# Squares, sums, taps and next norms placed elsewhere in the attention pair loop

## The chip, the cores and the metric

The kernel runs on one core of a Trainium2 chip. A core has five engines that each work through a queue of their own in order: TensorE (PE in the profile, its weight loads PEld), VectorE (DVE), ScalarE (ACT), GpSimd (POOL) and SyncE (SP), which issues the transfers. An engine stands still while the instruction at the head of its queue waits for another engine. The metric is the device time of one run in microseconds (us); the median of three runs is given.

## What is computed

The input is a batch of four images with 256 channels and 64 x 64 pixels. Four layers follow one another, each as `x = x + layer(group_norm(x))`. Layers 0 and 1 are attention layers, 2 and 3 Mamba layers. Cut to what matters here:

```python
def _gn(v, G=32, eps=1e-5):          # v's last axis is an image axis: 32 groups of 2 of its lines
    ...
    return ((g - m) / jnp.sqrt(s + eps)).reshape(v.shape)

# an attention layer
y = mhsa(x, ...)                     # a gated scan along the image
# ssa: 64 windows of 8 x 8 pixels; each window attends to its 4 most similar windows
attn = softmax(qh * SCALE @ kh)      # 8 heads, 64 queries x 256 keys per window
out = attn @ vh
lepe = depthwise_conv3x3(v_img) + lepe_b
out = (out + lepe) @ wo_w.T + wo_b
```

So a group of the norm is two neighbouring lines of the image (along its last axis) with all channels, and a strip of eight lines holds four groups and needs four means and four variances. The kernel keeps the image with these lines as its rows, and they are called rows below.

## The kernel before, in words

The partitions hold channels (2 x 128). The image is worked on in eight strips of eight rows. For each image the function `attention_layers` runs layer 0 and then layer 1, each as a scan phase (`scan_phase`) and a window phase (`window_phase`); the two Mamba layers follow. The order on every engine is the order in which the Python code emits instructions; nothing reorders them.

The window phase is a loop over 32 pairs of windows, `i = 4*sj + a`, with `sj` the strip and `a` from 0 to 3 the pair in it. A pair is handled in two halves h = 0 and 1 (its parity steps). Per half TensorE computes scores (L538), VectorE takes their minimum (L550), ScalarE the exponentials (L561, four per half, each with a sum), VectorE the reciprocal (L573), GpSimd four normalising multiplications (L576), TensorE transposes (L589), VectorE and ScalarE copy the transposes out (L600, L602), and TensorE forms the values (L615), a pair later. `own_rows` adds them into the image `vimg` on VectorE (L626). The halves of consecutive pairs are interleaved.

Around these, further work is hung into the loop:

- `project(s, m)`: the output projection of the finished strip `sj - 1`, at a = 1 and a = 2: four matmuls (L232) and, at the pair's end, an add into x on VectorE (L636). At pairs 19, 20, 23 and 24 a query projection of the same size stands there, which ScalarE copies out (L298).
- `taps`: the depthwise convolution of strips 6 and 7 on GpSimd, one step in each half of pairs 0 to 25: mostly a multiplication (`weigh`, L253) and then an addition (`add`, L256). The product lies in a buffer with the tag "sq", of which there is one.
- `dve_taps`: nine taps of strip 6 (channels 0 to 127) on VectorE (L268 the first, L270 the others), one at the end of each pair from 2 to 10.
- In layer 0 (`nxt` is set): the steps of the next layer's norm for strips 0 and 1 (`gn`): sums on VectorE (L143), their columns on TensorE (L134), the centring on GpSimd (L151), the square on ScalarE (L156, into the "sq" buffer), its reduction on VectorE (L160), the columns again, and the scaling (L167 on VectorE; L168, a power, and L172 on GpSimd).
- In layer 1: the variances of all eight strips (`stats`), which the Mamba layer needs: sums on VectorE (L200), columns on TensorE (L195), the mean on VectorE (L206), four squares on ScalarE (L215, one per group, each with a sum), columns, and a copy (L221). Strips 0 to 6 are hung into the loop, strip 7 follows it.

The dictionaries `mids` and `ends` hold what runs in the middle of a pair (after the first half's exponentials and the second half's minimum, before the second half's exponentials) and at its very end (before the next pair's first exponentials). `plan` fills them from a list of places; what falls past the last pair is returned in `left` and run after the loop, in an order written out by hand. In this phase all projections and all columns share the one PSUM buffer with the tag "mm".

Of the kernel before, what the change touches and what calls it, by code (L numbers as in the profile page):

```python
# [8 lines left out]
F32 = mybir.dt.float32  # L9
BF16 = mybir.dt.bfloat16  # L10
U32 = mybir.dt.uint32
AF = mybir.ActivationFunctionType
# [6 lines left out]
P = 128  # L19
NB = 4  # L20
C = 256
S = 64
# [22 lines left out]
class Net:  # L45
# [33 lines left out]
    def attention_layers(self, x, w_drams, v_drams):  # L79
        tc, nc = self.tc, self.nc  # L80
        with ExitStack() as ctx:
# [3 lines left out]
            norm = ctx.enter_context(tc.tile_pool(name="at_n", bufs=2, reuse_waits="tile"))  # L85
# [27 lines left out]
            def load_scan_weights(lay):  # L113
                lay["wa"] = wp.tile([P, 2, 4 * C], F32, tag="wa", name="att_wa")
                nc.sync.dma_start(lay["wa"], lay["w"][:, :, 0 : 4 * C])
# [73 lines left out]
            def stats(s, psum):  # L189
                xs = x.rearrange("p (c h w) -> p c w h", c=2, w=S)[:, :, strip[s], :]  # L190
                box = {}

                def columns(tag, part):
                    box[tag] = psum().tile([P, NT], F32, tag="mm", name=f"gn_{tag}")
                    nc.tensor.matmul(box[tag][:, 0:4], self.one_gn, part, start=True, stop=True)  # L195

                def sums():
                    box["s1"] = self.small.tile([P, 4], F32, tag="gn_s1", name="gn_s1")
                    xr = x.rearrange("p (n w) -> p n w", w=S)[:, :, strip[s]]
                    nc.vector.tensor_reduce(  # L200
                        box["s1"], xr.rearrange("p n (g t) -> p g n t", t=2), AX.XY, ALU.add
                    )

                def mean():
                    box["mean"] = self.small.tile([P, 4], F32, tag="gn_mean", name="gn_mean")
                    nc.vector.tensor_scalar(  # L206
                        box["mean"], box["pm"][:, 0:4], -1.0, None, ALU.mult
                    )

                def squares():  # L210
                    box["s2"] = self.small.tile([P, 4], F32, tag="gn_s2", name="gn_s2")
                    sq = norm.tile([P, 2, 8, S], F32, tag="xn", name="gn_sq")
                    for g in range(4):
                        two = slice(2 * g, 2 * g + 2)
                        nc.scalar.activation(  # L215
                            sq[:, :, two], xs[:, :, two], AF.Square,
                            bias=box["mean"][:, g : g + 1], accum_out=box["s2"][:, g : g + 1],
                        )

                def variance():  # L220
                    nc.vector.tensor_copy(self.gvar[:, 4 * s : 4 * s + 4], box["pv"][:, 0:4])  # L221

                return (
                    sums, lambda: columns("pm", box["s1"]), mean, squares,
                    lambda: columns("pv", box["s2"]), variance,
                )

# [241 lines left out]
            def window_phase(lay, work, psum, idx, nxt):  # L469
# [128 lines left out]
                def turned(h, j):  # L598
                    if j == 0:
                        nc.vector.tensor_copy(pts[h][0], pt[h][0])  # L600
                    else:
                        nc.scalar.activation(pts[h][1], pt[h][1], AF.Copy)  # L602
# [52 lines left out]
                dve_taps = lepe(lay, NW - 2)[:9]  # L655

                mids, ends, left = {}, {}, []
# [8 lines left out]
                if nxt:  # L666
                    load_scan_weights(nxt)
                    for s in range(2):
                        i = 10 + s
                        plan(gn(nxt, s, lambda: psum), (ends, i), (ends, i + 1), (mids, i + 2),  # L670
                             (ends, i + 2), (mids, i + 3), (ends, i + 5), (mids, i + 6))
                else:

                    for s in range(NW - 1):
                        i = 4 * s + 6
                        last = i + 6 if s < 5 else i + 3
                        plan(stats(s, lambda: psum), (ends, i), (ends, i + 1), (mids, i + 2),
                             (ends, i + 2), (ends, last), (mids, last + 1))
                for i in range(n_pair):
                    sj, a = divmod(i, 4)  # L680
                    add = evict = None
                    exps(i, 0, (0, 1))
                    if i:
                        scores(i, 1)
                        turned(0, 0)
                        turned(0, 1)
                        turn(i - 1, 1)
                        smallest(i, 1)
                    exps(i, 0, (2, 3))
                    for t in mids.get(i, ()):  # L690
                        t()
                    if i == 0:
                        for f in early:
                            f()
                    normalise(i, 0)
                    for t in taps[2 * i : 2 * i + 1]:
                        t()
                    if a == 3 and sj + 2 in (NW - 2, NW - 1):
                        evict = query(lay, sj + 2, 0, psum)
                    elif a == 0 and sj + 1 in (NW - 2, NW - 1):  # L700
                        evict = query(lay, sj + 1, 1, psum)
                    elif a in (1, 2) and sj:
                        add = project(sj - 1, a - 1, psum)
                    exps(i, 1, (0, 1))
                    scores(i + 1, 0)
                    if i:
                        turned(1, 0)
                        turned(1, 1)
                        values(i - 1)
                    turn(i, 0)  # L710
                    smallest(i + 1, 0)
                    exps(i, 1, (2, 3))
                    normalise(i, 1)
                    if i:
                        own_rows(i - 1)
                    for t in taps[2 * i + 1 : 2 * i + 2]:
                        t()
                    for t in dve_taps[i - 2 : i - 1] if i > 1 else ():
                        t()
                    if add:  # L720
                        add()
                    if evict:
                        evict()
                    gather(i + 3)
                    if a == 0 and 1 < sj + 1 < NW - 2:
                        double(sj + 1)
                    elif a == 1 and sj + 1 in (NW - 2, NW - 1):
                        double(sj + 1)
                    indices(i + 4)
                    for t in ends.get(i, ()):  # L730
                        t()
# [15 lines left out]
                box = {}  # L747
# [3 lines left out]
            with tc.tile_pool(name="at_p0", bufs=2, space=PSUM, reuse_waits="tile") as psum:  # L751
                box = {"psum": psum}
                g = [gn_four(layers[0], s, lambda: box["psum"]) for s in range(2)]
                for step in (g[0][0], g[1][0], g[0][1], g[0][2], g[0][3], g[1][1], g[1][2]):
                    step()
            tail = g[1][3:]
            for i, lay in enumerate(layers):
                with tc.tile_pool(name=f"at_a{i}", bufs=1, reuse_waits="tile") as work, tc.tile_pool(
                    name=f"at_p{i}", bufs=5, space=PSUM, reuse_waits="tile"
                ) as psum:  # L760
                    box["psum"] = psum
                    scan_phase(lay, work, psum, tail)
                    idx = routing(lay, work, psum)
                    taps = lepe(lay, NW - 3, psum)[:9]
                    for s in range(2, 5):
                        evicts = [query(lay, s, m, psum, nc.vector) for m in range(2)]
                        for t in taps[3 * s - 6 : 3 * s - 3]:
                            t()
                        for evict in evicts:
                            evict()  # L770
                    for t in lepe(lay, NW - 3, pool=True)[17:]:
                        t()
                with tc.tile_pool(name=f"at_c{i}", bufs=1, reuse_waits="tile") as work, tc.tile_pool(
                    name=f"at_q{i}", bufs=1, space=PSUM, reuse_waits="tile"
                ) as psum:
                    nxt = layers[i + 1] if i + 1 < len(layers) else None
                    box, tail, left = window_phase(lay, work, psum, idx, nxt)
                    if nxt is None:
                        box["psum"] = psum
                        g = stats(NW - 1, lambda: psum)  # L780
                        for t in (left[0], tail[0], left[1], tail[1], g[0], left[2], left[3], *g[1:]):
                            t()


# [1379 lines left out]
```

## Time and profile before

| what | value |
|---|---|
| median of three runs | 12,002.51 us (11,993.68 to 12,006.19) |
| the profiled execution, its own time | 11,985.03 us |
| its span | 11,983.3 us |
| busy: TensorE, VectorE, ScalarE, GpSimd | 84%, 82%, 58%, 74% of the span |
| granted TensorE clock, mean | 0.932 |
| squares of the variances (L215) | 128 x 0.766 us |
| GpSimd tap additions (L256) | 256 x 1.184 us |
| VectorE taps in the pair loop (L270) | 64 x 0.969 us |

A row of the costliest groups reads: line, engine, operation, tiles written and read, shapes, count; then busy time in us and mean ns of one; then how long the engine stood idle just before these instructions and what ended most of it. A row of a view of stretches reads: the stretch in us from the span's start, its length, busy time of each engine with its number of instructions, the granted TensorE clock (1.00 is full speed), and the transfers' share. A row of the timeline reads: start, duration, engine, line, operation, and in brackets the idle time before it with its releaser. A row of the waits reads: who waited for whom, total us, times, longest.

### The profile page before, as it was taken

The page shows a single profiled execution, that of the slowest core. Times are in us where ns is not written, and L with a number is a line of the kernel's source. Part 1 is how long each engine was busy: PE and PEld are TensorE (multiplying, and loading weights), DVE is VectorE, ACT ScalarE, POOL GpSimd, SP SyncE. Part 2 cuts the span into 40 slices and gives each one's busy share as a digit, 9 for nine tenths or more (in the row PEclk, how much of TensorE's full clock was granted, in tenths as well). Part 3 has the DMA queues.
Part 4 walks back from the last instruction along what each step waited for, and adds up shares of the span by engine and source line. Part 5 has one row for each costly group of instructions (what it writes and reads, how often), then busy time and mean ns, then how long its engine had stood idle before and what let it go on. Part 6 is the DMA issues. An engine that isn't in the chain of part 4 may idle for free.

```text
span 11983.3 us, 192241 instructions
## 1 busy us (share of the span) xinstructions
PE 10083.2 (84%) x71104; PEld 5778.2 (48%) x71104; DVE 9833.8 (82%) x8350; ACT 7002.3 (58%) x13096; POOL 8811.5 (74%) x6054
## 2 busy tenths in 40 slices
PE   8998887777899888777799988877778998887777
PEld 4564554444455455444445645544444554554444
DVE  6677998998666799899866779989986667998998
ACT  4555555776455555477645555547764555554776
POOL 4666886898456688689745668868984666887897
PEclk9999998999999899899999989989999999998999
DMA  3343454454334355445433434444543343454454
GB/s 96 100 126 134 174 175 149 169 180 160 92 98 127 134 173 177 145 169 182 159 90 99 128 132 173 174 148 167 180 160 91 100 127 135 173 176 146 169 176 154
DMA packets 682506, 1742.10 MB, mean 145 GB/s; under 512 B 88896, under 2 KB 194896, under 8 KB 681312
## 3 DMA queue, kind: packets, MB, share of 16 engines
q1 hardware_dynamic: 676448, 1721.41, 43.1%
q10 hardware_dynamic: 5120, 8.39, 0.3%
q8 instruction: 563, 9.22, 0.3%
q14 instruction: 375, 3.07, 0.1%
HBM read 1601.52 MB, written 94.39 MB: 142 GB/s over the span
## 4 chain that ended last, share of the span: by engine, by line
DVE 23%; PE 23%; ACT 8%; issue 5%; POOL 4%; DMA 1%; SPq 0%; DVEq 0%; POOLq 0%; ACTq 0%
DVE h L1002 13%; DVE pb L996 5%; PE conv_ps L232 4%; PE y L954 4%; PE u_ps L1291 3%; ACT da L938 2%; PE pb L926 1%; PE u_ps L1664 1%; POOL pr L576 1%; PE sc L538 1%; DVE lp L270 1%; PE pt_ps L589 1%; ACT dap L938 1%; PE z_ps L1316 1%; POOL hc L1008 1%
## 5 line engine op out<-in xcount | busy, mean ns | idle before, releaser
L1008 POOL TENSOR_TENSOR hc<-h,cb 128x1024 f32<-128x1024 f32 x2056 | 4809.6, 2350 | 806.4 <-DVE h L1002 350.9
L1002 DVE TENSOR_TENSOR_SCAN h<-da,m_state,pb 128x1024 f32<-128x1024 f32 x1248 | 2920.6, 2340 | 161.4 <-DVE pb L996 2.4
L954 PE MATMUL y<-ident,hc 128*128 128x128 f32 x16384 | 2333.6, 290 | 408.0 <-POOL hc L1008 340.9
L954 PEld LDWEIGHTS y<-ident,hc 128*128 128x128 f32 x16384 | 2034.5, 150 | 1124.9 <-POOL hc L1008 577.0
L996 DVE TENSOR_TENSOR pb<-du,pb 128x1024 f32<-128x1024 f32 x1672 | 2025.4, 1211 | 113.4 <-PE pb L926 110.9
L938 ACT ACTIVATE da<-delta,m_v 128x1024 f32<-128x1024 f32 x1672 | 1899.5, 1141 | 135.5 <-DVE h L1002 118.3
L926 PE MATMUL pb<-m_parts,pick 128*128 128x512 bf16 x3312 | 1078.2, 410 | 846.1 <-DVE h L1002 777.6
L576 POOL TENSOR_SCALAR pr<-pr,sm,zero 128x256 f32<-128x256 f32 x2048 | 1136.5, 569 | 476.8 <-DVE sm L573 475.8
L561 ACT ACTIVATE pr<-sc,mn 128x256 f32<-128x256 f32 x2048 | 955.9, 482 | 647.5 <-DVE sm L573 480.9
L926 PEld LDWEIGHTS <-pick 128*128 128x128 bf16 x3312 | 263.1, 101 | 1787.4 <-DVE h L1002 981.2
L550 DVE TENSOR_REDUCE mn<-sc 128x4 f32<-128x1024 f32 x512 | 627.9, 1228 | 550.0 <-PE sc L538 547.2
L1002 DVE TENSOR_TENSOR_SCAN h<-da,pb 128x1024 f32<-128x1024 f32 x424 | 969.5, 2287 | 55.1 <-DVE pb L996 0.9
L912 POOL TENSOR_TENSOR bb<-du,bb 128x1024 f32<-128x1024 f32 x376 | 888.6, 2363 | 88.8 <-DMA bb<-m_cd 84.0
L589 PE MATMUL pt_ps<-ident,pr 128*128 128x128 f32 x4096 | 705.4, 304 | 144.3 <-POOL pr L576 51.1
L1002 DVE TENSOR_TENSOR_SCAN h<-dap,m_state,bb 128x1024 f32<-128x1024 f32 x288 | 672.4, 2335 | 65.1 <-ACT dap L938 45.9
L232 PE MATMUL conv_ps<-att_y,att_wb 128*128 128x512 f32 x1536 | 683.3, 594 | 1.3 <-DVE gn_mean L206 1.3
L589 PEld LDWEIGHTS pt_ps<-ident,pr 128*128 128x128 f32 x4096 | 490.3, 151 | 307.5 <-POOL pr L576 161.7
L538 PE MATMUL sc<-kv,q_swap 32*64 32x128 f32 x8192 | 597.2, 287 | 6.7 <-DMA kv<-kv_dram 4.7
L938 ACT ACTIVATE dap<-delta,m_v 128x1024 f32<-128x1024 f32 x376 | 419.7, 1116 | 304.0 <-DVE h L1002 234.2
L538 PE MATMUL sc<-kv,att_y 32*64 32x128 f32 x7168 | 569.2, 287 | 11.8 <-DMA kv<-kv_dram 7.5
L538 PEld LDWEIGHTS sc<-kv,att_y 32*64 32x64 f32 x7168 | 430.0, 139 | 144.9 <-ACT pr L561 65.6
L270 DVE SCALAR_TENSOR_TENSOR lp<-vimg,att_v,lp 128x512 f32<-128x512 f32 x616 | 465.4, 756 | 28.1 <-DVE lp L270 1.4
(300 smaller groups left out, 17937.9 us busy)
## 6 DMA issues: line engine op xcount, KB each, us to landing
cb<-m_cd SPq DMA_DIRECT2D x2048, 512.0 KB, 3.8
kv<-kv_dram SPq DMA_DIRECT2D x1984, 128.0 KB, 2.8
bb<-m_cd SPq DMA_DIRECT2D x376, 512.0 KB, 5.4
kv_dram<-kst SPq DMA_DIRECT2D x128, 256.0 KB
kv_dram<-vn SPq DMA_DIRECT2D x128, 256.0 KB, 4.1
q_swap<-att_y SPq DMA_DIRECT2D x96, 256.0 KB, 4.3
m_pe<-in_pe_dram SPq DMA_DIRECT2D x32, 512.0 KB, 4.1
out_dram<-yo SPq DMA_DIRECT2D x64, 256.0 KB, 2.4
```

The lines of the kernel that those rows point to most:

```text
L232: nc.tensor.matmul(ps, w[:, k, w0 + m * P : w0 + (m + 1) * P], src[:, k], start=(k == 0), stop=(k == 1),)
L538: nc.tensor.matmul(sc[h][b * 64 : b * 64 + 64, r, w, m, :], (own(sj, m) if r == b else swap[sj % 2][:, m])[rows, 2 * a + w], kv[i, w][rows ...
L561: nc.scalar.activation(t[:, g].rearrange("p j r t -> p r j t"), sc[h][:, :, g // 2, g % 2, :].rearrange("p r (j t) -> p r j t", j=2), AF.E ...
L576: nc.gpsimd.tensor_scalar(t[:, g], t[:, g], s[:, g : g + 1], self.zero, ALU.mult, ALU.add)
L589: nc.tensor.transpose(pt[h][j][:, g, :], t[:, g, j].rearrange("p r t -> p (r t)"), self.ident,)
L912: nc.gpsimd.tensor_tensor(pb[i], slots[i][0]["du"], pb[i], ALU.mult)
L926: nc.tensor.matmul(pb[i][:, ss], self.pick[:, n : n + 1].to_broadcast([P, P]), blk["parts"][:, ss], start=True, stop=True,)
L938: nc.scalar.activation(da[i], blk["delta"], AF.Exp, scale=blk["a"](n))
L954: nc.tensor.matmul(blk["y"][:, ss], t[:, ss], self.ident, is_transpose=True, start=(n == 0 and ss.start % NT == 0), stop=(n == DS - 1 and ...
L996: nc.vector.tensor_tensor(pb[i], blk["du"], pb[i], ALU.mult)
L1002: nc.vector.tensor_tensor_scan(h[i][:, ss], da[i][:, ss], pb[i][:, ss], state, ALU.mult, ALU.add)
L1008: nc.gpsimd.tensor_tensor(hc[i][:, ss], h[i][:, ss], cb[i][:, ss], ALU.mult)
```

## The change

It moves steps in the window phase's loop; the instructions are the same ones.

- The four squares of a strip become four steps of their own: the first at the end of a pair with a = 1, the second and third in the middle and at the end of the pair with a = 2, the fourth in the middle of that with a = 3.
- The sums of a strip move from the end of a = 2 to the end of a = 3 (pairs 7, 11, ... 31); the second columns come four pairs after the sums, and the last variance step in the pair after.
- VectorE's nine taps move to the ends of pairs with a = 0 or 3 (pairs 3, 4, 7, 8, 11, 12, 15, 16 and 19). The ninth now stands after GpSimd's first taps of strip 7, which begin at pair 17 and write image rows 56 to 63; it reads rows 58 to 65.
- The next norm's strips 0 and 1 start at pairs 7 and 11 instead of 10 and 11; the square comes one pair after the centring instead of in the same pair.
- Strip 6 of the variances has its sums at the end of the last pair, so that its first columns and mean also run after the loop; the order there is rewritten.

```diff
-                def squares():
-                    box["s2"] = self.small.tile([P, 4], F32, tag="gn_s2", name="gn_s2")
-                    sq = norm.tile([P, 2, 8, S], F32, tag="xn", name="gn_sq")
-                    for g in range(4):
-                        two = slice(2 * g, 2 * g + 2)
-                        nc.scalar.activation(
-                            sq[:, :, two], xs[:, :, two], AF.Square,
-                            bias=box["mean"][:, g : g + 1], accum_out=box["s2"][:, g : g + 1],
-                        )
+                def square(g):
+                    if g == 0:
+                        box["s2"] = self.small.tile([P, 4], F32, tag="gn_s2", name="gn_s2")
+                        box["sq"] = norm.tile([P, 2, 8, S], F32, tag="xn", name="gn_sq")
+                    two = slice(2 * g, 2 * g + 2)
+                    nc.scalar.activation(
+                        box["sq"][:, :, two], xs[:, :, two], AF.Square,
+                        bias=box["mean"][:, g : g + 1], accum_out=box["s2"][:, g : g + 1],
+                    )
...
                 return (
-                    sums, lambda: columns("pm", box["s1"]), mean, squares,
+                    sums, lambda: columns("pm", box["s1"]), mean,
+                    *(lambda g=g: square(g) for g in range(4)),
                     lambda: columns("pv", box["s2"]), variance,
                 )
...
                 if nxt:
                     load_scan_weights(nxt)
                     for s in range(2):
-                        i = 10 + s
+                        i = 7 + 4 * s
                         plan(gn(nxt, s, lambda: psum), (ends, i), (ends, i + 1), (mids, i + 2),
-                             (ends, i + 2), (mids, i + 3), (ends, i + 5), (mids, i + 6))
+                             (ends, i + 3), (mids, i + 4), (ends, i + 4), (mids, i + 5))
                 else:
                     for s in range(NW - 1):
-                        i = 4 * s + 6
-                        last = i + 6 if s < 5 else i + 3
+                        i = 4 * s + 7
                         plan(stats(s, lambda: psum), (ends, i), (ends, i + 1), (mids, i + 2),
-                             (ends, i + 2), (ends, last), (mids, last + 1))
+                             (ends, i + 2), (mids, i + 3), (ends, i + 3), (mids, i + 4),
+                             (ends, i + 4), (mids, i + 5))
...
-                    for t in dve_taps[i - 2 : i - 1] if i > 1 else ():
-                        t()
+                    if a in (0, 3) and i and dve_taps:
+                        dve_taps.pop(0)()
...
-                        for t in (left[0], tail[0], left[1], tail[1], g[0], left[2], left[3], *g[1:]):
+                        var, left = left[0], left[1:]
+                        for t in (var, tail[0], left[0], left[1], tail[1], *left[2:6], g[0],
+                                  left[6], left[7], *g[1:]):
                             t()
```

## The prediction

> **What bounds the kernel now.** I read the summary page first. Its chain of waits (section 4) is led by the Mamba scans (L1002, L996, L954), which the edit does not touch; the attention pairs show only as L576 and L538 at 1% each. The edit can act only in the eight pair loops (four images, two layers), so I read those alone. Two page rows say who waits there:
>
> ```profile
> L576 POOL TENSOR_SCALAR pr<-pr,sm,zero 128x256 f32<-128x256 f32 x2048 | 1136.5, 569 | 476.8 <-DVE sm L573 475.8
> L561 ACT ACTIVATE pr<-sc,mn 128x256 f32<-128x256 f32 x2048 | 955.9, 482 | 647.5 <-DVE sm L573 480.9
> ```
>
> GpSimd's normalising and ScalarE's exponentials both wait for VectorE: no engine is saturated, the loop is a ring. So I cut it by pair, from the first exponential (L561) of one pair to that of the next, read off the instruction timeline, and asked the view of stretches for single pairs of image 1: layer 0's pairs 8, 10, 12, 17, then layer 1's pairs 8, 19, 20, 21, 22.
>
> ```profile
> core 0: us, PE busy (x) PEld busy (x) DVE busy (x) ACT busy (x) POOL busy (x), PEclk, DMA share, GB/s
> 3282.06:3289.01 6.95, 6.41 (x164) 4.98 (x153) 5.37 (x10) 5.00 (x21) 6.95 (x11) 1.00 0.45 138
> 3297.39:3305.28 7.89, 7.52 (x151) 5.06 (x149) 6.15 (x10) 4.83 (x18) 6.65 (x10) 1.00 0.47 148
> 3312.97:3327.84 14.87, 12.80 (x228) 10.35 (x216) 7.92 (x13) 5.92 (x21) 12.68 (x17) 0.73 0.49 151
> 3359.76:3373.51 13.75, 11.34 (x164) 8.12 (x154) 4.46 (x10) 4.94 (x19) 12.74 (x16) 0.75 0.42 125
> ...
> 3746.29:3756.72 10.43, 9.29 (x222) 7.93 (x210) 7.76 (x14) 7.73 (x28) 9.46 (x14) 0.89 0.42 128
> 3838.13:3846.43 8.30, 7.30 (x151) 5.04 (x149) 6.53 (x10) 5.41 (x20) 6.24 (x10) 1.00 0.41 128
> 3846.43:3855.44 9.01, 8.84 (x183) 6.65 (x184) 5.19 (x10) 8.22 (x28) 7.49 (x13) 1.00 0.43 136
> 3855.44:3861.82 6.38, 6.05 (x130) 3.95 (x121) 3.41 (x7) 4.75 (x21) 4.95 (x8) 1.00 0.51 148
> 3861.82:3869.04 7.22, 7.08 (x151) 5.01 (x149) 5.28 (x9) 4.84 (x19) 6.23 (x10) 1.00 0.64 191
> ```
>
> The last row is an undisturbed pair with a projection: 7.22 us, TensorE busy 7.08. The first has no projection: 6.95, GpSimd busy throughout. The others carry the steps that the edit moves. Layer 1's pair 8 holds four squares and takes 10.43 where layer 0's pair 8, without them, takes 6.95. Pair 20 holds four squares too. On ScalarE, pair 20's end and then pair 22's look like this:
>
> ```profile
> 3851.47 0.49 ACT L561 ACTIVATE pr<-sc,mn 128x256 f32<-128x256 f32 x1
> 3851.92 0.71 ACT L298 ACTIVATE att_y<-conv_ps,neg_bq 128x512 f32<-128x512 f32 x1
> 3852.49 0.80 ACT L215 ACTIVATE gn_sq<-x,gn_mean 128x256 f32<-128x256 f32 x1
> 3853.25 0.77 ACT L215 ACTIVATE gn_sq<-x,gn_mean 128x256 f32<-128x256 f32 x1
> 3853.98 0.77 ACT L215 ACTIVATE gn_sq<-x,gn_mean 128x256 f32<-128x256 f32 x1
> 3854.72 0.76 ACT L215 ACTIVATE gn_sq<-x,gn_mean 128x256 f32<-128x256 f32 x1
> 3855.44 0.50 ACT L561 ACTIVATE pr<-sc,mn 128x256 f32<-128x256 f32 x1
> ```
> ```profile
> 3865.21 0.47 ACT L561 ACTIVATE pr<-sc,mn 128x256 f32<-128x256 f32 x1 [0.97 <-DVE sm L573]
> ...
> 3869.04 0.47 ACT L561 ACTIVATE pr<-sc,mn 128x256 f32<-128x256 f32 x1 [1.41 <-DVE sm L573]
> ```
>
> Four squares, 0.74 apart, stand in front of the next pair's exponentials. An undisturbed pair leaves ScalarE idle twice, 0.97 in its middle and 1.41 at its end: one square fits each hole, four in one do not. Layer 0's stall is another one, from the waits:
>
> ```profile
> ACT gn_sq L156 <- POOL vimg L256: 12.8, 2, 6.5
> ```
>
> Twice a phase the next norm's square waits 6.4 us for GpSimd's tap, whose buffer it takes over.
>
> **Part 1, squares one per half pair (layer 1).** No instruction is added; the 24 squares of strips 0 to 5 are reordered inside the loop (strip 6's four run at the phase's end, before and after). Means over the four images, in groups of four pairs from a = 3, layer 1 against layer 0 where layer 0 has no norm steps (same attention work): pairs 7-10 35.0 against 29.8; 19-22 30.9 against 28.9; 23-26 30.9 against 28.9; 27-30 35.1 against 28.1. The difference is the price of the statistics: 5.2 + 2.0 + 2.0 + 7.0 = 16.2. For 11-14 (33.3) I take 7-10's 29.8 as the clean value: 3.5. For 15-18 (31.1), 29.0, between 28.1 and 29.8: 2.1. Pairs 3-6 have none. In all 21.8 us a phase, and it contains VectorE's sums, the half clock that stalls bring (0.89 in pair 8's row), and a 1.0 us wait in pair 30, where the columns of strip 5 want the one "mm" PSUM buffer while VectorE still adds from it (pair 29); in the new order they come at pair 31.
> What stays: a square at the end (0.74 in 1.41) costs nothing; one in the middle (0.74 in 0.97) nothing to 0.1. Bounds: 0 each, or 0.95 each if the hole were already the ring's slack. I take 0.05 x 24 = 1.2, being nearest to the measured holes.
>
> **Part 2, sums on a = 3.** Seven reductions of 1.22 us. Now they follow the add (1.37 on VectorE) of a = 2; pair 19 shows it: 8.30 against 7.22. After, they follow an end without an add, but at pairs 7, 11, 15, 19 a tap (0.97) stands before them. VectorE's chain from one reciprocal to the next is then 0.17 + 0.40 + 0.97 + 1.22 + 0.69 + 1.23 to the exponentials of the second half, which need about 2.5 with the copy between: 7.2. Against 6.95 that costs 0.3, against 6.3 (GpSimd's own load: 8 x 0.54 + 1.18 + 0.77) 0.9. I take 0.4 x 4 = 1.6. Queued behind the sums: the PSUM copy and the next minimum, and through it both ScalarE and GpSimd. Layer 1 nets -21.8 + 1.2 + 1.6 = **-19.0 a phase**.
>
> **Part 3, VectorE's nine taps.** They run at the end of a pair, hence in the next interval: now in intervals 3 to 11, after in 4, 5, 8, 9, 12, 13, 16, 17, 20. So "pairs without a projection" is only half true: taps at a = 0 fall into a = 1, which projects, and 20 has a query projection. The price in a projecting interval is 7.89 - 7.22 = 0.67 (second row against the last); elsewhere the 0.43 by which one normalising step stretches beside a tap (four take 2.59 instead of 2.16). Before, 4 x 0.67 + 5 x 0.43 = 4.8; after, 5 x 0.67 + 4 x 0.43 = 5.1: +0.3. The Trainium skill (SBUF — State Buffer, section "Who interferes with whom") says that a VectorE instruction with two SBUF inputs and a GpSimd one that reads SBUF exclude each other for the whole instruction. By it a tap may hold GpSimd for all its 0.97, which speaks against this move, as four taps now land in layer 0's intervals 12, 13, 16, 17, where GpSimd is busy 12.7 of 13.75 to 14.87: 3.9 a phase, against 4 x 0.43 = 1.7 by the row. I take the row's 1.7 as the dearer place, so +1.0 in layer 0.
> The ninth tap (pair 19) now reads rows that GpSimd's strip-7 taps write from pair 17 on: a new wait of VectorE on GpSimd's add of pair 19's first half. That add ends about 6.5 into an undisturbed pair, the tap starts about 7.5 into it, so 0; at most one add, 1.18, with the sums and the next minimum behind it.
>
> **Part 4, next norms (layer 0).** GpSimd's work stays: centre 2.47, power 1.65, scale 1.90, twice: 12.0 a phase. Now it falls into pairs 12, 13, 16, 17. The groups 11-14 and 15-18 take 42.9 + 34.1 against 29.8 + 29.0: 18.2. After, the strips are four pairs apart; centres at 9 and 13 lie beside projections, where GpSimd has about 1 us free (7.22 - 6.23), and the following pair again: 4 of 12.0 hidden. The square, a pair later than its centre, still waits for the tap's add: in pair 10 that add ends 3.8 after the next pair's start, 3.4 without the tap's stall. With 1.06 for the square, less about 1.1 that the next pair makes up (20 is followed by 6.38), that is 3.4 x 2 = 6.8. Sum 12.0 - 4 + 6.8 = 14.8 against 18.2: -3.4, with the taps **-2.4 a phase**. Bounds: -12 (GpSimd's backlog drained in between) and +5 (nothing hidden, each square at its full 4.5).
>
> **Part 5, the phase's end.** Strip 6's columns and mean now stand between the two last projections, which share the one "mm" buffer: about 0.4 + 0.15 and two handovers, +0.75. Its sums move from pair 30 to 31, which takes 1.2 out of pair 31; they lie beside the last normalising (2.2). Net -0.5.
>
> **The sum.** 4 x (-19.0 - 2.4 - 0.5) = -87.6. The profiled run took 11,985.0 (span 11,983.3 and 1.7 around it), 17.5 below the median of 12,002.5; -87.6 on the median gives **11,915**.
>
> **Rivals.** (A) As above, 0.62, 11,870 to 11,950. (B) More: the half clock goes in layer 0 as well (0.73 and 0.75 in its rows) and GpSimd's backlog drains: -12 there, -23 in layer 1: 4 x -35 = -140, 11,860. For it: every undisturbed row shows 1.00. Against: the squares' wait stays. 0.13. (C) Half: the holes fill only partly, layer 1 gives -11 and layer 0 +3: 4 x -8 = -32, 11,970. For it: the middle hole leaves 0.2 us. 0.17. (D) Slower: each spread square costs its whole 0.95 (0.74 and the accumulator read), because exponentials, minimum and scores are a ring in which any ScalarE delay in a pair's middle stays: 24 x 0.95 = 22.8 against the 21.8 removed, with layer 0 at its bound: 4 x (22.8 - 21.8 + 1.6 + 5 - 0.5) = +28, 12,031. It turns slower from about 0.65 us a square with layer 0 there. Against it: pair 20, four squares long (2.95), is only 1.8 over 7.22. 0.08. That the edit doesn't do what it says holds for the taps alone, and is in the sum.
>
> **Numbers.** Predicted 11,915; range 11,850 to 11,975 (B to C, without D). A run of this kernel can tell 0.2% (24 us) from no change: faster (under 11,978) 0.86, from A, B and most of C; same 0.07, slower 0.07.
>
> **What would show it.** Right: layer 1's pair 8 near 7.3, 20 and 24 near 7.5, 28 near 6.7; no pair with four L215 in a row but the phase's end; layer 1's loops shorter by some 19 us, layer 0's by 2 or 3; L156 still waiting for L256, about 4.5 a time. Wrong: ScalarE's middle exponentials late by a square in every pair; taps' intervals 13, 17, 20 above 8.5; or layer 0's pairs 9 to 17 longer in sum than now.

## The result, and the profile after

The changed kernel takes 11,910.4 us (median of 4 runs, 11,902.7 to 11,913.1) against 12,000.3 before (4 runs): ratio 0.9926, 95% interval 0.9912 to 0.9941. The forecast was 11,915. The profiled execution took 11,902.7, with a span of 11,901.0.

Cut into pairs as in the prediction (first exponential to first exponential, means over the four images), the loop of layer 1 fell from 247.5 to 225.4 us, that of layer 0 from 246.8 to 246.0. Four times the sum, 4 x (22.1 + 0.8) = 91.6, covers the whole gain (89.9 between the medians, 82.3 between the two profiled executions). Layer 1 gave a little more than forecast, layer 0 nothing that can be told from scatter. For such a mean comes from one profiled execution: layer 0's loop, whose code is the same in the changed kernel and in three of the runs below, reads 246.0, 247.8, 248.4 and 246.9. A difference between two loops of under some 2.5 us is therefore not a finding by itself.

The half clock fell along with layer 1's loop: TensorE was granted half its clock for 44.4 us of it before and for 15.0 us after (mean of the four images). How much of the 22.1 us the clock itself gave, no run here separates.

| pairs | layer 0 before | after | layer 1 before | after |
|---|---|---|---|---|
| 3-6 | 33.1 | 29.2 | 29.9 | 28.7 |
| 7-10 | 29.8 | 34.6 | 35.0 | 28.5 |
| 11-14 | 42.9 | 39.0 | 33.3 | 28.0 |
| 15-18 | 34.1 | 35.8 | 31.1 | 28.7 |
| 19-22 | 28.9 | 29.3 | 30.9 | 30.9 |
| 23-26 | 28.9 | 28.9 | 30.9 | 29.8 |
| 27-30 | 28.1 | 27.3 | 35.1 | 28.5 |

The view of stretches for single pairs of image 1, changed kernel: layer 0's pairs 10, 12, 13, 17, then layer 1's pairs 8 and 22 (columns as before; the last three numbers are granted clock, transfers' share, GB/s).

```profile
3282.45:3295.07 12.62, 9.94 (x191) 6.90 (x190) 8.77 (x12) 5.91 (x19) 10.63 (x17) 1.00 0.51 150
3300.97:3307.92 6.95, 6.36 (x165) 5.16 (x158) 5.98 (x10) 4.81 (x18) 5.83 (x7) 0.94 0.51 145
3307.92:3322.32 14.40, 11.54 (x170) 8.41 (x159) 5.74 (x11) 4.97 (x21) 13.45 (x17) 0.76 0.38 117
3347.26:3362.33 15.07, 12.65 (x168) 8.14 (x157) 5.67 (x10) 4.97 (x21) 11.01 (x16) 0.66 0.38 107
...
3734.38:3741.34 6.96, 6.12 (x160) 4.62 (x148) 6.20 (x9) 4.87 (x21) 6.70 (x11) 1.00 0.55 168
3836.68:3843.90 7.22, 7.08 (x151) 5.00 (x149) 5.29 (x9) 6.34 (x23) 6.23 (x10) 1.00 0.64 182
```

Layer 1's pair 8 has come down from 10.43 to 6.96, at full clock. Pair 22 now holds two squares (ScalarE busy 6.34 instead of 4.84) and still takes 7.22. In layer 0 the long pairs have only moved: 12 is short, but 10, 13, 14 (mean 11.61, before 8.05) and 17 are now the long ones, and 17, which holds one scale where it held two, is longer than before (15.07 against 13.75), at a clock of 0.66.

On ScalarE, the middle and the end of layer 1's pair 10 (the timeline; the exponentials are L562 now):

```profile
3752.25 0.77 ACT L215 ACTIVATE gn_sq<-x,gn_mean 128x256 f32<-128x256 f32 x1
3753.36 0.47 ACT L562 ACTIVATE pr<-sc,mn 128x256 f32<-128x256 f32 x1 [0.24 <-DVE sm L574]
...
3755.64 0.80 ACT L215 ACTIVATE gn_sq<-x,gn_mean 128x256 f32<-128x256 f32 x1
3757.18 0.47 ACT L562 ACTIVATE pr<-sc,mn 128x256 f32<-128x256 f32 x1 [0.64 <-DVE sm L574]
```

Each square lies in the hole and leaves a rest (0.24 and 0.64) in which ScalarE still waits for VectorE. That is the picture the prediction drew. Layer 0's square still waits for the tap, 5.2 a time instead of 6.4:

```profile
ACT gn_sq L156 <- POOL vimg L257: 10.4, 2, 5.6
```

One part of the computation differs in the changed kernel: the ninth tap reads image rows 58 to 63 after GpSimd has written strip 7's result there, so its share of strip 6 is another one. It is the same in every run below that keeps the ninth tap at pair 19.

### The profile page after: what moved, and what is told of

The parts are those of the page before. It is cut to its first block, busy times and chain, and to the rows that moved or that the text cites. A ratio compares the mean times of both kernels' runs of the same rounds, so it can differ in the third digit from the quotient of the medians.

```text
span 11901.0 us, 192257 instructions
## 1 busy us (share of the span) xinstructions
PE 10079.7 (85%) x71104; PEld 5762.7 (48%) x71104; DVE 9822.4 (83%) x8350; ACT 7006.9 (59%) x13096; POOL 8811.2 (74%) x6054
## 5 line engine op out<-in xcount | busy, mean ns | idle before, releaser
L562 ACT ACTIVATE pr<-sc,mn 128x256 f32<-128x256 f32 x2048 | 952.7, 477 | 551.1 <-DVE sm L574 368.9
L551 DVE TENSOR_REDUCE mn<-sc 128x4 f32<-128x1024 f32 x512 | 629.3, 1230 | 516.9 <-PE sc L539 515.7
L590 PE MATMUL pt_ps<-ident,pr 128*128 128x128 f32 x4096 | 673.6, 296 | 105.2 <-POOL pr L577 57.6
```

The source lines that it names most:

```text
L562: nc.scalar.activation(t[:, g].rearrange("p j r t -> p r j t"), sc[h][:, :, g // 2, g % 2, :].rearrange("p r (j t) -> p r j t", j=2), AF.E ...
L590: nc.tensor.transpose(pt[h][j][:, g, :], t[:, g, j].rearrange("p r t -> p (r t)"), self.ident,)
```

## The experiments

The theory to test was the prediction's: a square alone fits ScalarE's hole, four in a row do not. The main rival was that the place, not the number, decides. In each diff the lines with "-" are those of the kernel named, and "..." marks a cut. Each ratio is to the kernel before, timed again beside its group of runs (medians 11,992.8 to 12,005.7), so runs of different groups are compared by their ratios and their loops.

**Parts alone.** First the squares, on the kernel before, as four steps like those of the change (only strip 5's second columns move too, by one pair):

```diff
-                        last = i + 6 if s < 5 else i + 3
+                        last = i + 6 if s < 5 else i + 4
                         plan(stats(s, lambda: psum), (ends, i), (ends, i + 1), (mids, i + 2),
-                             (ends, i + 2), (ends, last), (mids, last + 1))
+                             (ends, i + 2), (mids, i + 3), (ends, i + 3), (mids, i + 4),
+                             (ends, last), (mids, last + 1))
```

> The kernel before with the four squares of a strip as four half-pair steps (ends of a = 0, middle and end of a = 1, middle of a = 2), strip 5's second columns one pair later; sums, taps and norms as before. Theory H (holes: a square alone fits ScalarE's idle time, four do not): layer 1's loop shorter by 14 to 18 us a phase, the rest untouched, -56 to -72 us in all, about 11,935. Rival P (place: what counts is that sums and columns left the pairs with an add): at most -5 a phase, about 11,980.

Measured: 11,975.5, ratio 0.9975 (0.9964 to 0.9986); layer 1's loop 239.6. That is -7.9 a phase: half of what the theory wanted, more than the rival. Of the 7.9, 4.1 are in pairs 27-30, where the columns of strip 5 also lost their wait. Pairs 7-10 gave 2.2; in 11-14 to 23-26 the groups stayed within 0.3 of before. Spreading from the old place, with the sums where they were, is not the whole gain.

Then the taps alone, the changed kernel's `if a in (0, 3)` in the kernel before:

```diff
-                    for t in dve_taps[i - 2 : i - 1] if i > 1 else ():
-                        t()
+                    if a in (0, 3) and i and dve_taps:
+                        dve_taps.pop(0)()
```

> The kernel before with VectorE's taps alone moved to a = 0 and 3 (the ninth then reads rows that GpSimd's strip-7 taps have begun to overwrite, so that part of the convolution differs). The record's step (the same nine taps, five in projecting intervals instead of four): +0.3 a phase in layer 1, +1 in layer 0, about +5 us in all. Rival T (a tap in an interval that also has the add is much dearer than one without): -2 to -3 a phase, about -20 us.

Measured: 11,985.9, ratio 0.9986 (0.9978 to 0.9995); layer 1 -3.6 a phase, layer 0 -2.1. The total agrees with rival T, and so do single intervals: 6 and 10 of layer 0, which have the add and lost their tap, fell from 8.44 and 7.89 to 7.23 each. Interval 20, with a tap and a query projection, rose by 0.43, and 17 by 1.25. Layer 0's -2.1 is within the scatter.

Then the next norms alone:

```diff
-                        i = 10 + s
+                        i = 7 + 4 * s
                         plan(gn(nxt, s, lambda: psum), (ends, i), (ends, i + 1), (mids, i + 2),
-                             (ends, i + 2), (mids, i + 3), (ends, i + 5), (mids, i + 6))
+                             (ends, i + 3), (mids, i + 4), (ends, i + 4), (mids, i + 5))
```

> The kernel before with the next layer's norms alone moved to pairs 7 to 16. The record's step: layer 0's loop -3.4 a phase, about -14 us in all. Rival S (spread over four stalls instead of two, each stall drops TensorE to half clock, which makes the next pair long): +1 to +4 a phase, +4 to +16 us, with intervals 13 and 17 near 14.

Measured: 12,004.3, ratio 0.9999 (0.9991 to 1.0008); layer 0's loop 247.2 against 246.8. The norms' move is worth nothing. Intervals 10, 13, 14 and 17 took 13.5, 14.2, 11.7 and 12.3: four long pairs, 13 near the 14 that rival S named but 17 not, and layer 0's half clock grew from 42.7 to 50.3 us; but the +1 to +4 a phase that S forecast did not come clear of the scatter.

**Number or place.** The changed kernel with the four squares together again, at the end of a = 1:

```diff
-                             (ends, i + 2), (mids, i + 3), (ends, i + 3), (mids, i + 4),
+                             (ends, i + 2), (ends, i + 2), (ends, i + 2), (ends, i + 2),
                              (ends, i + 4), (mids, i + 5))
```

> The changed kernel with the four squares of a strip together again, at the end of a = 1. Theory H: layer 1's loop is 10 to 15 us a phase longer than in the changed kernel (six strips, 1.8 to 2.5 us each), about 11,960. Rival P: no more than 3 a phase, about 11,920.

Measured: 11,914.7, ratio 0.9921 (0.9904 to 0.9937); layer 1's loop 226.5, 1.1 above the changed kernel and within the scatter. Rival P is right and my theory of the number fell: four squares in a row cost next to nothing there. Why shows in ScalarE's hole at the end of a pair. In the kernel before, layer 0, where no squares disturb but VectorE's taps run, its first exponentials of pairs 6, 8 and 9 (timeline) show the hole at the end of a = 1, 3 and 0:

```profile
3267.61 0.47 ACT L561 ACTIVATE pr<-sc,mn 128x256 f32<-128x256 f32 x1 [2.54 <-DVE sm L573]
...
3282.06 0.50 ACT L561 ACTIVATE pr<-sc,mn 128x256 f32<-128x256 f32 x1
3289.01 0.47 ACT L561 ACTIVATE pr<-sc,mn 128x256 f32<-128x256 f32 x1 [0.82 <-DVE sm L573]
```

Here the hole is 2.54 after a = 1, 0.8 after a = 0, none after a = 3, and 1.2 after a = 2 (pair 7). It is not the same all along the loop: before pairs 21 to 24 of the same layer, after a = 0, 1, 2 and 3, it is 1.1, 1.7, 1.4 and 0.8. So the better witness is the changed kernel's own layer 1. Its first exponentials of pairs 13, 14 and 21, that is, after a = 0, after a = 1 with a square in front, and after a = 0 again:

```profile
3769.52 0.50 ACT L562 ACTIVATE pr<-sc,mn 128x256 f32<-128x256 f32 x1
3777.89 0.47 ACT L562 ACTIVATE pr<-sc,mn 128x256 f32<-128x256 f32 x1 [1.44 <-DVE sm L574]
...
3829.05 0.47 ACT L562 ACTIVATE pr<-sc,mn 128x256 f32<-128x256 f32 x1 [1.44 <-DVE sm L574]
```

After a = 0 the hole is none before pairs 13 and 17 and 0.3 before 29, but 1.4 before 21 and 25, which follow a query projection. After a = 1 some 1.4 is left beside a square with its accumulator read (about 0.95), so about 2.3 by estimate, and four squares (2.95) nearly fit. Before, the squares stood after a = 0. To test it, the same block after a = 0 in the changed kernel, which for strips 0 to 4 is three pairs later (their second columns follow later too):

```diff
+                        j = i + 5 if s < 5 else i + 2
+                        last = i + (8 if s < 4 else 7 if s == 4 else 4)
...
-                             (ends, i + 2), (mids, i + 3), (ends, i + 3), (mids, i + 4),
-                             (ends, i + 4), (mids, i + 5))
+                             (ends, j), (ends, j), (ends, j), (ends, j),
+                             (ends, last), (mids, last + 1))
```

> The changed kernel with the four squares of strips 0 to 4 together at the end of a = 0, three pairs later than in the run with all four at the end of a = 1 (11,915); their second columns follow later too. Theory L (the hole's length at that place decides: none or 0.9 at the end of a = 0, 2.6 at the end of a = 1): five strips, 1.8 to 3.5 each, +8 to +16 us a phase in layer 1 against that run, 11,945 to 11,980. If any end is as good: 11,915.

Measured: 11,928.4, ratio 0.9942 (0.9925 to 0.9958); layer 1's loop 232.8 against 226.5. Five strips cost 6.3, less than forecast; the totals' intervals overlap (0.9904 to 0.9937 with the block after a = 1), but the loop's difference is beyond the scatter. It is not 1.3 for each strip. Summed over the block's pair and the two that follow it, pairs 12-14, 16-18 and 28-30 are 2.7, 1.8 and 2.1 longer than with the block after a = 1, 20-22 and 24-26 0.3 shorter. The block costs where the hole is none or 0.3, and costs nothing where it is 1.4: theory L holds, place by place. Layer 1's pairs 12 and 13 in this run, with the block in 12, and in the run with the block after a = 1, which has it in 13:

```profile
3760.08:3769.66 9.58, 8.32 (x202) 6.66 (x190) 8.12 (x14) 7.75 (x28) 9.58 (x15) 1.00 0.55 166
3769.66:3778.01 8.35, 6.67 (x112) 4.86 (x113) 3.06 (x7) 4.87 (x21) 4.61 (x7) 0.80 0.52 158
```
```profile
3765.35:3772.02 6.67, 6.00 (x160) 4.79 (x150) 6.00 (x10) 4.85 (x21) 6.67 (x10) 1.00 0.50 145
3772.02:3781.08 9.06, 8.67 (x178) 6.31 (x166) 5.81 (x12) 7.80 (x28) 8.07 (x14) 1.00 0.63 176
```

**The sums.** The changed kernel with the sums back behind the add:

```diff
-                        plan(stats(s, lambda: psum), (ends, i), (ends, i + 1), (mids, i + 2),
+                        plan(stats(s, lambda: psum), (ends, i - 1), (ends, i + 1), (mids, i + 2),
```

> The changed kernel with the sums of the variances back at the end of a = 2, behind the add; the squares stay spread. If the sums' place matters (the middle hole of a = 3 grew by 1.2 to 2.1 where sums and add stood together): layer 1's loop +1 to +1.5 for each of six strips, +6 to +9 a phase, about 11,940. The record's price is 0.8 to 1 each less 0.4, +3 a phase, 11,922. If only the squares matter: 11,910.

Measured: 11,950.9, ratio 0.9959 (0.9945 to 0.9973); layer 1's loop 234.1, +8.7. So the sums' place is the dearest single part of the change that was put back alone. In layer 1's pair 11 of this run VectorE does add, sums, copy and minimum in one row (L637 to L551), and ScalarE, even with a square in front, waits 1.54 in the middle of the pair; the same hole is 0.3 in the changed kernel. These 1.3 more recur in all six strips of the measured loop and make 7.6 of the 8.7.

```profile
3767.28 1.38 DVE L637 SCALAR_TENSOR_TENSOR x<-conv_ps,att_v,x 128x512 f32<-128x512 f32 x1
3768.68 1.22 DVE L200 TENSOR_REDUCE gn_s<-x 128x4 f32<-128x1024 f32 x1
...
3771.73 0.47 ACT L562 ACTIVATE pr<-sc,mn 128x256 f32<-128x256 f32 x1 [1.54 <-DVE sm L574]
```

**Taps elsewhere.** The changed kernel with all nine taps in intervals without a projection:

```diff
-                    if a in (0, 3) and i and dve_taps:
+                    if (a in (2, 3) or i == 1) and dve_taps:
```

> The changed kernel with VectorE's taps at the ends of pairs 1, 2, 3, 6, 7, 10, 11, 14, 15, so that each falls into an interval without a projection, and the ninth stands before GpSimd's strip-7 taps. Theory (the tap is charged where it runs, in the next interval): intervals 5, 9, 13, 17, 20 shorter by 0.5 to 1.2, intervals 3, 7, 11, 15 longer by 0.4 to 0.9, net -1 to -4 us a phase in both layers, about 11,890. Rival (a tap costs the same everywhere): within 5 us of 11,910.

Measured: 11,894.8, ratio 0.9916 (0.9899 to 0.9932), not to be told from the changed kernel's; layer 1's loop 226.0, layer 0's 245.6. The single steps came as expected (interval 20 8.57 to 7.68, 9 8.63 to 8.21; 7 5.78 to 7.07, 11 5.76 to 6.77), but they cancel, as far as the scatter lets one see: a tap behind the add costs what a tap beside a projection does. The ninth tap now stands ahead of GpSimd's strip-7 taps again, here and in every later run with the taps in these places.

**Where layer 0's gain went.** The changed kernel with the next norm's square in a dead strip of y instead of the taps' buffer:

```diff
-                    box["sq"] = norm.tile([P, 2, 8 * S], F32, tag="sq", name="gn_sq", bufs=1)
+                    if free:
+                        box["sq"] = y[:, :, strip[s], :].rearrange("p c w h -> p c (w h)")
+                    else:
+                        box["sq"] = norm.tile([P, 2, 8 * S], F32, tag="sq", name="gn_sq", bufs=1)
```

> The changed kernel with the next norm's square written into a finished strip of y instead of the buffer that GpSimd's taps use, so that it waits for the centring alone. Theory W (the square's wait for the tap is what keeps layer 0 from gaining): layer 0's intervals 10 and 14 fall from 12.6 and 11.6 to about 8.5, its loop by 6 to 8 us a phase, about 11,882. Rival G (GpSimd's own 12 us of norm work and the half clock after it set the time; the square waits beside it): under 2 us a phase, about 11,905.

Measured: 11,859.0, ratio 0.9882 (0.9866 to 0.9898); layer 0's loop 237.6, -8.4. Theory W holds. Its pairs 10 and 13 in layer 0:

```profile
3280.67:3288.89 8.22, 7.62 (x151) 5.19 (x151) 5.48 (x9) 5.89 (x19) 7.32 (x12) 1.00 0.61 163
3302.23:3317.04 14.81, 12.31 (x167) 8.64 (x157) 5.82 (x11) 4.94 (x21) 13.50 (x17) 0.65 0.47 134
```

Pair 10 is mended (12.62 to 8.22), 13 is not. So the changed kernel without GpSimd's power and scale (the two strips stay unscaled):

```diff
                     nc.vector.tensor_scalar(rstd, pv, 1e-5, None, ALU.add)
+                    if bare:
+                        return
```

> The changed kernel without GpSimd's power and scale of the next norm in layer 0's window phase (the two strips go on centred but not scaled). Theory C (a stall of one scale costs its 3.55 us of GpSimd and then about 2.5 us because TensorE falls to half clock while it waits): intervals 13 and 17 fall from 14.5 and 14.7 to about 9 and 8.4, 11 to 13 us a phase, with some 20 us less half clock. Rival (GpSimd's time alone): 3.6 each, 7 us a phase, the half clock as before.

Measured (one run): 11,848.0. Layer 0's pairs 13 and 17 of this run:

```profile
3291.14:3299.52 8.38, 8.02 (x168) 5.66 (x156) 5.13 (x11) 4.97 (x21) 8.38 (x11) 1.00 0.51 150
3324.74:3333.13 8.39, 7.98 (x168) 5.63 (x157) 5.08 (x10) 4.97 (x21) 7.47 (x12) 1.00 0.55 160
```

Means: 14.51 to 8.38 and 14.67 to 8.38, 6.1 and 6.3 where GpSimd's own time is 3.55; 11.6 a phase, with the half clock per layer-0 loop down from 42.7 us to 25.6. That is what theory C forecast. While the normalising waits behind the scale, TensorE has nothing to do; in the changed kernel's pair 17 it stands idle for 2.24, is then granted half its clock, and the projection takes 3.62 instead of 1.88 in an undisturbed pair (TensorE's timeline):

```profile
3349.75 2.93 PE L590 MATMUL pt_ps<-ident,pr 128*128 128x128 f32 x8 [2.24 <-POOL pr L577]
...
3356.29 3.62 PE L233 MATMUL conv_ps<-vimg,att_wb 128*128 128x512 f32 x4
```

Delay and half clock went away together here, so that the clock makes the rest, 2.6 and 2.7, is inferred. It is large enough for it: by the rows of pairs 13 and 17 the half clock lasted 6.9 and 10.2 us (14.40 x 0.24 x 2 and 15.07 x 0.34 x 2), in which TensorE can fall behind by half of that.

**A better version.** First the two edits above in one kernel, the square's buffer and the free taps:

> The changed kernel with both single edits that were run before it: the next norm's square in a finished strip of y, and VectorE's taps at pairs 1, 2, 3, 6, 7, 10, 11, 14, 15. If they add up: layer 0's loop about 237 us, layer 1's about 225, 11,845 to 11,860. If the taps at 12 and 16 were part of the two long intervals 13 and 17 (GpSimd stretched by a tap just when it is late): layer 0's loop 2 to 4 us shorter than with the square alone, 11,840.

Measured: 11,872.2, ratio 0.9893 (0.9877 to 0.9910); layer 0's loop 240.5, layer 1's 224.1. They do not add up: not faster than the square alone. Then, in this kernel, the norms moved to where GpSimd has no more taps:

```diff
-                        i = 7 + 4 * s
-                        plan(gn(nxt, s, lambda: psum, free=True), (ends, i), (ends, i + 1), (mids, i + 2),
-                             (ends, i + 3), (mids, i + 4), (ends, i + 4), (mids, i + 5))
+                        at = (23, 25, 26, 26, 27, 27, 28) if s == 0 else (24, 28, 29, 29, 30, 30, 31)
+                        plan(gn(nxt, s, lambda: psum, free=True), *zip(
+                            (ends, ends, mids, ends, mids, ends, mids), at))
```

> As the run with the own square buffer and the free taps, and the next norms' steps at pairs 23 to 31, most of them after GpSimd's last tap (pair 25), where it has about 2.9 us free beside a projection. Theory (GpSimd's centre and scale are dear because GpSimd is full while it has taps): layer 0's loop 227 to 231 us instead of about 237, intervals 13 and 17 near 8.3 and 7.9, the last pairs +1 to +3 in all, 11,815 to 11,830. Rival (the stall only moves): 11,850.

Measured: 11,862.0, ratio 0.9895 (0.9878 to 0.9911); layer 0's loop 231.8, but the way from its last pair to layer 1's first grew from 218.9 to 223.8, so only some 4 us a phase are left of 8.7, and the total doesn't tell it from the run before. Intervals 13 and 17 did fall, from 13.83 and 13.90 to 7.95 each, but 29 took 13.95. So GpSimd's taps are not all of the reason: here it has none left, stands idle right in front of the power, waiting for VectorE's middle step (which ends with the reciprocal that the row names), and then runs power and scale ahead of the normalising (GpSimd, layer 0's pairs 28 and 29 of this run):

```profile
3406.23 1.65 POOL L171 TENSOR_TENSOR gn_rstd<-gn_rstd,minus_half 128x8 f32<-128x8 f32 x1 [1.27 <-DVE sm L577]
3407.96 1.90 POOL L175 TENSOR_TENSOR att_xn<-att_xn,gn_rstd 128x1024 f32<-128x1024 f32 x1
3409.84 4.33 POOL L580 TENSOR_SCALAR pr<-pr,sm,zero 128x256 f32<-128x256 f32 x8
```

Last, the kernel just shown with GpSimd's three steps (centre, power, scale) issued one step after what they wait for:

```diff
-                        at = (23, 25, 26, 26, 27, 27, 28) if s == 0 else (24, 28, 29, 29, 30, 30, 31)
+                        at = ((20, 23, 24, 25, 26, 27, 27, 28, 28, 29) if s == 0 else
+                              (21, 24, 25, 26, 27, 28, 28, 29, 30, 31))
...
-                            (ends, ends, mids, ends, mids, ends, mids), at))
+                            (ends, ends, mids, ends, ends, mids, ends, mids, ends, ends), at))
```

The ten places are sums, columns, mean, centre, square, reduction, columns, VectorE's part of the scaling, power, scale. The run thus differs in two more things: the steps begin three pairs earlier, and power and scale stand apart.

> As the run with late norms, but GpSimd's centre, power and scale are issued one step after the VectorE copies that they need, at the ends of pairs 25 to 31, power and scale apart. In the late run GpSimd stood idle 2.3 to 2.8 us in front of the centre and the power, waiting for VectorE's middle step, and then ran them ahead of the normalising. Theory Q (what counts is whether the work can start in that idle time): centre and scale lie in it, interval 29 falls from 13.95 to about 8.5, layer 0's loop from 231.8 to 224 to 227, 11,835 to 11,850. Rival (any 2 to 3.6 us on GpSimd before a normalising stalls the ring): the cost is spread over 26 to 31, loop 230 or more, 11,860.

Measured: 11,842.0, ratio 0.9861 (0.9840 to 0.9881); layer 0's loop 226.9, and no growth behind it (219.2). This beats the kernel before by 1.4%, and its profiled loop of layer 0 is the shortest of all; the totals of this run and the one before it just touch (0.9881 and 0.9878). Its pairs 26 and 29 in layer 0, and GpSimd in pair 26, around the first centre:

```profile
3377.24:3384.41 7.17, 7.02 (x150) 4.95 (x148) 5.23 (x9) 5.79 (x19) 6.78 (x9) 1.00 0.64 172
3398.10:3405.95 7.85, 7.48 (x153) 5.40 (x152) 4.27 (x9) 4.91 (x18) 6.01 (x10) 1.00 0.61 180
```
```profile
3377.34 2.18 POOL L606 TENSOR_SCALAR pr<-pr,sm,zero 128x256 f32<-128x256 f32 x4 [1.04 <-DVE sm L603]
3379.48 2.48 POOL L183 TENSOR_TENSOR att_xn<-x,gn_mean 128x1024 f32<-128x1024 f32 x1
3381.93 2.18 POOL L606 TENSOR_SCALAR pr<-pr,sm,zero 128x256 f32<-128x256 f32 x4
```

The centre starts the moment the normalising ends, with no wait in front. The next normalising, whose reciprocal was ready at 3380.6, starts 1.3 later, right behind it; so most of the centre lies in the idle time, and the pair keeps its 7.2 and the full clock. That fits theory Q. What the earlier start and the parting of power and scale add to it was not tried apart.

## Why the prediction was right, and where its steps were off

- **Part 1 (squares).** The size was right, its split was not. I priced all of layer 1's statistics at 21.8 and the loop lost 22.1, but I let nearly all of it hang on four squares in a row. Lined up, the runs share it out: 247.5 before, 243.9 with the taps alone moved, 232.8 with the sums and columns moved too but the squares of five strips still in a row after a = 0, 225.4 in the changed kernel. So the squares' part is 7.4, and 6.3 of that comes with the block moved whole to a = 1 (226.5). I had measured ScalarE's hole in one pair, with a = 2, and took it for all; it is the hole at the block's place that decides, and cutting the block up is one way out of a bad place.
- **Part 2 (sums).** Mis-sized: by the record's prices a net gain of about 3 stood in the expectation of the run that puts them back; it measured 8.7. The term that was too small is the chain add, sums, copy, minimum, on which ScalarE's middle hole of a = 3 hangs. The price I set on the new place, 1.6, is of the right order in sum but sits elsewhere: by the means, pairs 8, 12 and 16 took 6.86, 6.75 and 6.71, no more than the undisturbed 6.95, and pair 20 took 8.57 where I gave 7.5.
- **Part 3 (taps).** Sign wrong for the move alone: I priced +0.3 and +1.0, it measured -3.6 in layer 1 and -2.1, within the scatter, in layer 0. In an interval with an add but no projection layer 1 paid 1.3, 1.0 and 0.7 for a tap (7, 11 and 15 of the run with the free taps) where I charged 0.43; layer 0 paid nothing there, so that the price of a tap stays half open. How +1.0 follows from 1.7 against 3.9 I did not work out, and layer 1's +0.3 never entered the sum. My remark that a = 0 is no place without a projection was true and without weight, as the two prices cancel. The half-blocked normalising (0.43) was the right row: in the changed kernel's pairs 13 and 17 four normalising steps beside a tap take 2.60 again, and the tap itself, behind GpSimd's scale, 1.36 and 1.37. A block of GpSimd for the tap's whole time, which the rule allows, was not seen.
- **Part 4 (norms).** This part failed: -3.4 forecast, +0.4 alone, -0.8 for layer 0 with the taps. My own sign of being wrong came true: layer 0's pairs 9 to 17 took 88.9 in sum, 84.7 before. That the loop is not longer is luck of the profiled execution: its pairs 0 to 8 took 67.7 before and 64.4 after, but 65.6 in the run with the squares spread, whose layer 0 is that of the kernel before. The square's wait was priced 3.4, and measured about 4.4 (12.59 to 8.19 and 11.61 to 7.27 without it). Power and scale were priced at their own 3.55 with a part hidden; nothing was hidden, and they measured 6.1 to 6.3. Rival B had hoped for full clock in layer 0; the half clock stayed at 42.7 us a loop against 42.7 before (mean of the four).
- **Part 5.** Last pair's start to the Mamba layer's first step: 25.9 to 26.8 before, 24.8 to 26.0 after; nothing to see, as forecast.

So the total came out within 5 us because layer 1's 3 too little and layer 0's 1.6 too much stand against each other, which is luck; the forecast's case A was the right one, and its picture of layer 1 was half right.

## What to carry to other kernels

Measure an engine's idle time at every place of a periodic loop, not at one: here ScalarE had none to 1.4 us after a = 0 and some 2.3 after a = 1, and moving a block whole to the right place did nearly as much (6.3) as cutting it up and moving its parts (7.4). Background work in an engine's queue was cheapest here with its inputs there before the idle time began; issued together with the step that it waits for, it ran behind the idle time and ahead of the loop's own work.

## What was not expected of the hardware

A delay of 3.55 us on GpSimd cost 6.1 to 6.3 a pair. In those pairs TensorE, after standing without work, was granted half its clock for 7 to 10 us (a mean of 0.76 and 0.66 over the pair), and at full clock without the delay. That the clock makes the difference is the likely reading; no run holds the delay and takes the half clock away.
